# A third turn buffer and three reorderings in an adaLN attention and FFN block

## The chip, the cores and the metric

The kernel runs on one core of a Trainium2 chip. Time is the device time of one execution in microseconds (us), lower is better. All arithmetic is float32.

## The reference

Eight batches (B = 8) of 1024 rows with 256 columns pass through a modulated attention and a modulated feed-forward network, each added back to the row.

```python
mod = (_silu(L0_c) @ L0_wmod).reshape(L0_c.shape[0], 6, 1, -1)
sa, ca, ga, sb, cb, gb = (mod[:, j] for j in range(6))
ga = (2 * (ga >= 0) - 1) * jnp.maximum(jnp.abs(ga), 0.25)     # gb likewise
h = _layernorm(x, axis=-1) * (1 + ca) + sa
scores = jnp.einsum('nsd,ntd->nst', h * w_lhs, h * w_rhs)
x = x + ga * jnp.einsum('nst,ntd->nsd', softmax(scores, axis=2), h)
h = _layernorm(x, axis=-1) * (1 + cb) + sb
x = x + gb * (relu(h @ W1 + b1) @ W2 + b2)
```

## The kernel before

**Tiles and stages.** A batch has eight row tiles of 128 rows (`NT = 8`). The main loop (line 1140) goes over batches `b` and stages `i` from 0 to 7. Stage `i` finishes the attention of row tile `i` of batch `b`, computes the scores of tile `i + 2` (`ahead`), and runs a quarter of the FFN of the half batch that was finished earlier (`fb`, `fg`). Stages 0, 1, 4 and 5 (`first`) do the first FFN product for two pairs of column blocks each, `c` and `c + 1`. Stages 2, 3, 6 and 7 do the second FFN product (`y_first`, `y_second`) and the attention product of two row tiles together (`pair_begin`, `pair_end`). Products over pairs replace eight block products by seven and some sums. The FFN of the last half batches follows in a closing loop (line 1343).

**What sets the order.** `pin` ties each instruction to the one before it on its engine, so that every engine executes its instructions in the order in which the code names them. Engines wait for each other by semaphores that follow from the data and from the reuse of tiles. A tile with `bufs=n` can be written again when all readers of the tile n allocations earlier are done; transfers that read it count as readers. DMAs are issued by SP (`nc.sync`) in order, some loads by ACT.

**Names around the change.** Engines are PE (matmul), DVE (vector), ACT (scalar), POOL (GpSimd) and SP.

- Scores: `direct` (psc, L410) computes one half of the symmetric part; `mirror` (L433) turns it by blocks of 32 on DVE into a tile T (named Tm), and `move` writes T to DRAM (D_m, L304) and reads it back turned (L307).
- T is one tag for four users: the mirrored scores (Tm), the turned norms for attention (T_a) and FFN (T_f, both L320), and the FFN result (T_y, L853). It has two buffers, the number of the pool `two`.
- Softmax: `row_max` (m, L460, DVE), `max_turn` (pm, L465, a PE transpose of the maximum), `subtract` (pT, L472, DVE), `exponent` (pT, L481, ACT), then `product` (po, L493) or the pair products (pp, L544; pq, pr, L584).
- Sides: `prepare_turn_apart` (rT and lT, L340, ACT) makes the next batch's two score operands from X_a, the turned T_a.
- First FFN product: `pair_products` makes pa, pb and pc (L718) and keeps a copy of pa in SBUF (`kept`, L737, ACT, three buffers); `between`, called after pb, is where `max_turn` is put. `pair_sums` (L752 to L761) and `pair_last` add them on DVE (L769) and POOL (L770); `pair_last` first writes one more product over the left half of pa. `pair_relu` (L779, L780) and `pair_turn` (L789 to L792) follow.
- Statistics: `pair_stats` takes mean and variance of two row tiles on DVE (L239, L240), `ffn_rstd` the reciprocal deviation on ACT (rb, L245, L246).

In a stage of the first kind, the order in the code is: `direct(ahead)`, `pair_products(c)` with `max_turn(late)` in it, `pair_sums(c)`, `mirror(ahead)`, `pair_last(c)`, in stage 4 the turn T_a of the next batch, `subtract(late)`, `pair_products(c + 1)`, in stage 5 the next sides, the ReLUs, `exponent(late)`, `pair_sums(c + 1)`, `pair_last(c + 1)`, `row_max(ahead)`. `late` is the tile whose scores were completed in the stage before; in stage 5 it is tile 6.

Of the kernel before, what the change touches and what calls it, by code (L numbers as in the profile page):

```python
# [11 lines left out]
F32 = mybir.dt.float32  # L12
# [5 lines left out]
P = 128  # L18
# [6 lines left out]
def adaln_block_kernel(  # L25
# [14 lines left out]
    B, S, D = x.shape  # L40
    INTER = W1.shape[1]
    NT = S // P
    ND = D // P
    NI = INTER // P
    HALF = 512
    TH = HALF // P
    H2 = HALF // 2
    NH = NI // 2
    V = 32
    NV = P // V  # L50
# [3 lines left out]
    two = ctx.enter_context(tc.tile_pool(name="two", bufs=2))  # L54
    work = ctx.enter_context(tc.tile_pool(name="work", bufs=3))
# [67 lines left out]
    w1 = const.tile([P, ND, INTER], F32, name="w1")  # L123
# [14 lines left out]
    def warm(n):  # L138
# [9 lines left out]
            name=nc.get_next_instruction_name(),  # L148
# [88 lines left out]
    def stats(mv, t, src, name):  # L237
        st = work.tile([P, nc.vector.BN_STATS_DIM], F32, tag="st", name=f"st_{name}")
        nc.vector.bn_stats(st, src)  # L239
        nc.vector.bn_aggr(mv[:, t, :], st)  # L240

    def rstd_of(mv, tag, name):

        r = work.tile([P, TH], F32, tag=tag, name=name)
        nc.scalar.activation(r, mv[:, :, 1], AF.Ln, bias=eps)  # L245
        nc.scalar.activation(r, r, AF.Exp, scale=-0.5)  # L246
        return r
# [50 lines left out]
    def move(out, blocks, m, name, hurry=True):  # L298


        D_ = dram.tile([NV, V, NV, NT * V], F32, tag="D", name=f"D_{name}", bufs=3)
        D_ = D_[:, :, :, 0:m]
        for a in range(NV):
            nc.sync.dma_start(  # L304
                out=D_[:, :, a, :].rearrange("b u m -> u b m"), in_=blocks[ts(a, V)]
            )
        read = lambda: nc.sync.dma_start(out=out, in_=D_.rearrange("b u a m -> (b u) a m"))  # L307
        if hurry:
            read()
            read_back()  # L310
        else:
            reads.append(read)

    def turn_blocks(src, name, X=None):

        T = two.tile([P, NV, NT * V], F32, tag="T", name=f"T_{name}")
        for k in range(ND):
            nc.vector.transpose(  # L320
                T.rearrange("p b (k t v) -> p k b t v", k=ND, v=V)[:, k],
                src(k).rearrange("p t (b v) -> p b t v", v=V),
            )
        if X is None:
            X = two.tile([P, NV, NT * V], F32, tag="X", name=f"X_{name}", bufs=1)
        move(X, T, NT * V, name)
        return X.rearrange("p a (k t v) -> p k t a v", k=ND, v=V)
# [6 lines left out]
    def prepare_turn_apart(b, g, side):  # L334

        tag = "lr"[side] + "T"
        T = two.tile([P, ND, HALF], F32, tag=tag, name=f"{tag}_{b}_{g}", bufs=2)
        (lT_t, rT_t)[side][b, g] = T
        for k in range(ND):
            nc.scalar.activation(  # L340
                T[:, k, :].rearrange("p (t a v) -> p t a v", a=NV, v=V),
                pre[b, g][:, k], AF.Identity,
                scale=side_col(side, 0, k, b), bias=side_col(side, 1, k, b),
            )
# [77 lines left out]
    def mirror(b, i):  # L422
        if i == NT - 1:
            return
        n = NT - 1 - i
        if b == 0:
            mirror_first(i)
            return
        T = two.tile([P, NV, NT * V], F32, tag="T", name=f"Tm_{b}_{i}")
        T = T.rearrange("p b m -> p (b m)")[:, : NV * n * V].rearrange(  # L430
            "p (b m) -> p b m", b=NV
        )
        nc.vector.transpose(  # L433
            T.rearrange("p b (j v) -> p b j v", v=V),
            sc_t[b][:, i + 1 :, :, i, :].rearrange("p j b v -> p b j v"),
        )
        move(
            sc_t[b][:, i, :, i + 1 :, :].rearrange("p a j v -> p a (j v)"), T, n * V,
            f"m{b}_{i}",
        )  # L440
# [39 lines left out]
    def exponent(b, i):  # L480
        nc.scalar.activation(pT_t[b, i], pT_t[b, i], AF.Exp)  # L481
# [134 lines left out]
    def pair_stats(b, i):  # L616
        two_t.pop((b, i))
        g, j = divmod(i, TH)
        for q in range(2):
            stats(mvb_t[b, g], j + q, x_tile(b, i + q), f"b{b}_{i + q}")  # L620
# [15 lines left out]
    def ffn_rstd(b, g):  # L636
        mv = mvb_t.pop((b, g))
        ffn["r", g] = mv, rstd_of(mv, "rb", f"rb_{b}_{g}")
# [75 lines left out]
    lo, hi = slice(0, H2), slice(H2, HALF)  # L714
    pairs = {}

    def mm(out, lhsT, rhs):
        nc.tensor.matmul(out, lhsT=lhsT, rhs=rhs, start=True, stop=True)  # L718

    def pair_products(b, g, c, between=None):  # L720

        if c == 0:
            ffn["f"] = two.tile([P, NI, HALF], F32, tag="f", name=f"f_{b}_{g}", bufs=1)
            if b < B - 1:
                ffn["ft"] = two.tile([P, 3, NH, H2], F32, tag="ft", name=f"ft_{b}_{g}", bufs=1)
        hT, hs = ffn["hT", g]
        n = ts(c, P)
        s1, a22 = (w1[:, k, ds((c + NH) * P, P)] for k in range(2))

        pool, tag = (ps_s, "s") if b == B - 1 else (ps_a, "a")  # L730
        pa = ps_a.tile([P, HALF], F32, tag="a", name=f"pa_{b}_{g}_{c}")
        pb = pool.tile([P, HALF], F32, tag=tag, name=f"pb_{b}_{g}_{c}")
        pc = ps_a.tile([P, HALF], F32, tag="a", name=f"pc_{b}_{g}_{c}")
        mm(pa[:, lo], w1[:, 0, n], hT[:, 0, lo])
        mm(pa[:, hi], s1, hs[:, 0])
        kept = work.tile([P, HALF], F32, tag="kept", name=f"kept_{b}_{g}_{c}", bufs=3)
        nc.scalar.copy(kept, pa)  # L737
        mm(pb[:, lo], w1s[:, 0, n], hs[:, 1])
        mm(pb[:, hi], w1s[:, 1, n], hs[:, 2])
        if between:  # L740
            between()
        mm(pc[:, lo], w1[:, 1, n], hT[:, 1, lo])
        mm(pc[:, hi], a22, hT[:, 0, hi])
        pairs[c] = pa, pb, pc, kept

    def pair_sums(b, g, c):
# [16 lines left out]
    def pair_last(b, g, c):  # L763


        pa, kept, u = pairs.pop(c)
        f = ffn["f"]
        mm(pa[:, lo], w1s[:, 2, ts(c, P)], ffn["hT", g][0][:, 1, hi])
        nc.vector.tensor_tensor(f[:, c, hi], pa[:, lo], u, ALU.add)  # L769
        nc.gpsimd.tensor_tensor(  # L770
            f[:, c::NH, hi],
            f[:, c::NH, hi],
            kept[:, None, hi].to_broadcast([P, 2, H2]),
            ALU.add,
        )
# [72 lines left out]
    def y_turn(b, g, hurry=False):  # L848

        Y = ffn["Y"]  # L850
        T = two.tile([P, NV, NT * V], F32, tag="T", name=f"T_y{b}_{g}")
        for h in range(2):
            nc.vector.transpose(  # L853
                T.rearrange("p a (t h u) -> p a t h u", h=2, u=V)[:, :, :, h, :],
                Y[:, h].rearrange("p (t a v) -> p a t v", a=NV, v=V),
            )
        Y = Y.rearrange("p h r -> p (h r)").rearrange("p (b m) -> p b m", b=NV)
        move(Y, T, NT * V, f"y{b}_{g}", hurry)
        ffn["rows", b, g] = Y.rearrange("p b (t h u) -> p t h b u", h=2, u=V)
# [279 lines left out]
    late = None  # L1139
    for b in range(B):  # L1140
        for i in range(NT):
# [6 lines left out]
            c = i % TH * 2  # L1148

            if (b, i) == (0, NT - 2):  # L1150
# [11 lines left out]
                late, last_exponent = ahead, None  # L1162
# [38 lines left out]
            if first:  # L1201
# [3 lines left out]
                pair_products(fb, fg, c, turn_max)  # L1205
                if i == 0:
                    ffn_rstd(b - 1, 1)
                elif (b, i) == (B - 1, TH):
                    ffn_rstd(b, 0)
                if (b, i) == (1, 0):  # L1210
                    weights(*late)
                    late = None
# [3 lines left out]
                if ahead:  # L1216
                    mirror(*ahead)
                pair_last(fb, fg, c)
                if i == 0 and back:
                    for q in range(2):  # L1220
                        y_add(ub, ug, q)
# [5 lines left out]
                if late:  # L1227
                    subtract(*late)
                pair_products(fb, fg, c + 1, (lambda: max_turn(*extra)) if extra else None)
                if i == 5 and b + 1 < B:  # L1230
                    prepare_turn_apart(b + 1, 1, 1)
                    prepare_turn_apart(b + 1, 1, 0)
                pair_relu(c)
                sides_too = i == 4 and b + 1 < B
                if sides_too:
                    prepare_turn_apart(b + 1, 0, 1)
                if late:
                    exponent(*late)
                if sides_too:
                    prepare_turn_apart(b + 1, 0, 0)  # L1240
# [80 lines left out]
            if first:  # L1321
                product(b, i)
                product_out(b, i)
            elif half and ahead:
                pair_end(b, i - 1)
                pair_out(b, i - 1)
                if i < NT - 1:
                    y_turn(fb, fg)
                if i == NT - 1:
                    assert not queue  # L1330
                    right_sums(b + 1, range(3))
                if i == NT - 1 or b == B - 1:
                    pair_stats(b, i - 1)
            late = ahead if ahead != extra else None
            if first and back:
# [6 lines left out]
    b = B - 1  # L1342
# [75 lines left out]
```

## Time and profile before

| what | value |
|---|---|
| median of 3 runs | 772.51 us (772.37 to 774.09) |
| profiled execution | 774.46 us, its span 772.7 us |
| granted TensorE clock | 1.0 of full speed throughout |
| PE busy | 759.6 us in 3708 matmuls |
| DVE busy | 565.1 us |
| POOL busy | 538.2 us |
| ACT busy | 375.4 us |
| DMA | 95.18 MB, 123 GB/s on the mean |

The profile is of one execution, recorded by the hardware. A line of the timeline gives the start and the duration of a group of equal instructions, the engine, the line of the kernel, the operation, what it writes and reads, the shape, and in brackets how long the engine had been idle before and whose end released it. Ends of matmuls are modelled; their starts are recorded. The second number of a waits row is how often, the third how long the longest was.

### The profile page before, as it was taken

To read this page: it belongs to the slowest core of one execution; us is meant where nothing else is said; L and a number is where in the kernel's file an instruction comes from. 1 tells how busy PE (TensorE), PEld (TensorE's weight loads), DVE (VectorE), ACT (ScalarE), POOL (GpSimd) and SP (SyncE) were. 2 spreads that over 40 slices of the span, in tenths; PEclk is the share of its full clock that TensorE was granted. 3 is DMA by queue.
4 is the path that set the end of the run, shared out by engine and by line. 5 is a ranking of instruction groups with operands and counts; after the bars stand their busy time and mean duration, and the time that the engine had idled before them with its cause. 6 is when DMAs were issued, how large, how long until landed. Compare 5 with 4: busy or idle time off the path is not lost.

```text
span 772.7 us, 11479 instructions
## 1 busy us (share of the span) xinstructions
PE 759.6 (98%) x3708; PEld 621.8 (80%) x3708; DVE 565.1 (73%) x1222; ACT 375.4 (49%) x681; POOL 538.2 (70%) x632
## 2 busy tenths in 40 slices
PE   8999999999999999999999999999999999999998
PEld 3576788788887888778887888878888788889886
DVE  6697878768785887758787687876878677595632
ACT  3464546635456355645546444563546535251511
POOL 4543974978849686596867787497884969559641
PEclk9999999999999999999999999999999999999999
DMA  5314335356443554434543554436534254142220
GB/s 193 123 50 145 106 103 133 101 176 170 123 122 101 171 143 113 140 95 151 156 126 118 150 150 130 117 101 192 167 93 130 87 167 142 35 115 98 81 83 27
DMA packets 106211, 95.18 MB, mean 123 GB/s; under 512 B 29700, under 2 KB 98848, under 8 KB 106152
## 3 DMA queue, kind: packets, MB, share of 16 engines
q1 hardware_dynamic: 98408, 85.81, 38.0%
q10 hardware_dynamic: 7744, 8.65, 3.7%
q8 instruction: 29, 0.48, 0.3%
q14 instruction: 30, 0.25, 0.1%
HBM read 50.62 MB, written 43.81 MB: 122 GB/s over the span
## 4 chain that ended last, share of the span: by engine, by line
PE 78%; DVE 10%; POOL 4%; DMA 3%; issue 2%; SPq 1%; ACT 1%; DVEq 0%; POOLq 0%
PE psc L410 14%; PE po L493 12%; PE pa L718 7%; PE yc L796 6%; PE ya L796 6%; PE yb L796 6%; PE pc L718 5%; PE pr L584 5%; PE pb L718 4%; PE pq L584 3%; PE py L901 3%; PE yd L796 3%; PE pp L544 3%; DMA D_y<-T_y 2%; DVE pT L472 1%
## 5 line engine op out<-in xcount | busy, mean ns | idle before, releaser
L770 POOL TENSOR_TENSOR f<-f,kept 128x512 f32<-128x512 f32 x64 | 81.5, 1273 | 116.7 <-DVE f L769 84.6
L410 PE MATMUL psc<-rT,lT 128*128 128x512 f32 (+3 forms) x384 | 134.6, 487 | 0.0
L493 PE MATMUL po<-xg,pT 128*128 128x257 f32 x576 | 131.6, 380 | 0.0
L493 PEld LDWEIGHTS po<-xg,pT 128*128 128x128 f32 x576 | 108.9, 190 | 15.9 <-issue 1.0
L472 DVE TENSOR_TENSOR pT<-sc,pm 128x1024 f32<-128x1024 f32 x64 | 77.1, 1205 | 30.7 <-PE pm L465 24.8
L410 PEld LDWEIGHTS psc<-rT,lT 128*128 128x128 f32 x384 | 67.7, 191 | 37.9 <-issue 26.3
L417 ACT COPY sc<-psc 128x512 f32<-128x512 f32 (+3 forms) x96 | 44.9, 475 | 104.0 <-PE psc L410 94.5
L481 ACT ACTIVATE pT<-pT 128x1024 f32<-128x1024 f32 x64 | 67.3, 1052 | 33.8 <-DVE pT L472 33.8
L460 DVE TENSOR_REDUCE m<-sc 128x1 f32<-128x1024 f32 x64 | 77.3, 1207 | 0.0
L737 ACT COPY kept<-pa 128x512 f32<-128x512 f32 x64 | 37.4, 584 | 78.2 <-PE pa L718 78.2
L779 ACT ACTIVATE f<-f 128x512 f32<-128x512 f32 x64 | 40.1, 627 | 62.4 <-POOL f L770 62.4
L718 PE MATMUL pb<-hs,w1s 128*128 128x256 f32 x256 | 66.0, 380 | 0.9 <-DVE f L755 0.8
L718 PE MATMUL pc<-hT,w 128*128 128x256 f32 x256 | 65.8, 380 | 0.0
L634 POOL TENSOR_TENSOR x<-x,rows 128x256 f32<-128x256 f32 x64 | 45.3, 739 | 22.3 <-DVE x L509 11.8
L718 PEld LDWEIGHTS pb<-hs,w1s 128*128 128x128 f32 x256 | 47.8, 190 | 9.1 <-DVE f L755 2.0
L718 PEld LDWEIGHTS pc<-hT,w 128*128 128x128 f32 x256 | 46.7, 192 | 6.9
L796 PE MATMUL yc<-f,w2s 128*128 128x256 f32 x224 | 52.1, 379 | 0.0
L796 PEld LDWEIGHTS yc<-f,w2s 128*128 128x128 f32 x224 | 41.5, 190 | 10.1 <-issue 2.9
L433 DVE STREAM_TRANSPOSE Tm<-sc 128x896 f32<-128x896 f32 (+6 forms) x49 | 34.6, 707 | 13.3 <-ACT sc L417 12.4
L790 POOL TENSOR_TENSOR ft<-ft,f 128x256 f32<-128x256 f32 x56 | 40.8, 728 | 4.4
L791 POOL TENSOR_TENSOR ft<-ft,f 128x256 f32<-128x256 f32 x56 | 40.8, 728 | 4.4
L789 POOL TENSOR_TENSOR ft<-f 128x256 f32<-128x256 f32 x56 | 40.9, 731 | 0.0
(165 smaller groups left out, 1672.7 us busy)
## 6 DMA issues: line engine op xcount, KB each, us to landing
D_f<-T_f SPq DMA_DIRECT2D x60, 128.0 KB, 2.7
X_f<-D_f SPq DMA_DIRECT2D x15, 512.0 KB, 3.7
D_a<-T_a SPq DMA_DIRECT2D x56, 128.0 KB, 3.2
D_y<-T_y SPq DMA_DIRECT2D x56, 128.0 KB, 2.6
Y<-D_y SPq DMA_DIRECT2D x14, 512.0 KB, 3.5
out_dram<-x SPq DMA_DIRECT2D x14, 512.0 KB, 3.0
X_a<-D_a SPq DMA_DIRECT2D x13, 512.0 KB, 3.4
x<-in_L_attn_x_dram ACTq DMA_DIRECT2D x12, 512.0 KB, 4.6
```

The source lines that it names most:

```text
L410: nc.tensor.matmul(psc[:, : hi - lo], lhsT=lT_t[b, i // TH][:, k, ts(i % TH, P)], rhs=rT_t[b, n][:, k, lo - n * HALF : HALF], start=(k == ...
L417: nc.scalar.copy(score_row(b, i)[:, lo // V : hi // V, :], psc[:, : hi - lo].rearrange("p (n v) -> p n v", v=V),)
L460: nc.vector.tensor_reduce(m, score_row(b, i), AX.XY, ALU.max)
L472: nc.vector.tensor_tensor(pT.rearrange("p j (a v) -> p j a v", v=V), score_columns(b, i), pm[:, :P].rearrange("p (j a v) -> p j a v", j=1, ...
L481: nc.scalar.activation(pT_t[b, i], pT_t[b, i], AF.Exp)
L493: nc.tensor.matmul(po[:, : D + 1], lhsT=pT[:, t, :], rhs=xg_t[b][:, t, 0 : D + 1], start=(t == 0), stop=(t == NT - 1),)
L584: nc.tensor.matmul(out, lhsT=lhs[:, t, :], rhs=rhs[:, t, :], start=(t == 0), stop=(t == TH - 1),)
L634: queue.append(lambda: nc.gpsimd.tensor_tensor(out, in0, row, op))
L718: nc.tensor.matmul(out, lhsT=lhsT, rhs=rhs, start=True, stop=True)
L770: nc.gpsimd.tensor_tensor(f[:, c::NH, hi], f[:, c::NH, hi], kept[:, None, hi].to_broadcast([P, 2, H2]), ALU.add,)
L789: add(ft[:, 0, c], f[:, c + NH, hi], f[:, c, hi], ALU.subtract)
L796: nc.tensor.matmul(out, lhsT=lhs(c), rhs=rhs(c), start=(c == 0), stop=(c == NH - 1))
```

## The change

Five edits. The tag T gets three buffers in all of its uses. In `pair_products`, `between` is called after both pc products and not ahead of them. In stage 5, `exponent(late)` stands ahead of the next batch's sides. In the last batch, the statistics of tiles 2 and 3 and the reciprocal deviation of the first half stand in stage 4 behind the first pair's sums; before, the statistics stood at the end of stage 3, and the deviation ahead of the sums. To make room, `kept` has two buffers for three, and in the last batch's own FFN (the closing loop) the third pair of each four (c = 2) uses the tile `s1`.

```diff
 # turn_blocks, mirror, y_turn
-        T = two.tile([P, NV, NT * V], F32, tag="T", name=...)
+        T = two.tile([P, NV, NT * V], F32, tag="T", name=..., bufs=3)
 # pair_products
-        kept = work.tile([P, HALF], F32, tag="kept", name=f"kept_{b}_{g}_{c}", bufs=3)
+        tag, bufs = ("s1", 1) if b == B - 1 and c % 3 == 2 else ("kept", 2)
+        kept = work.tile([P, HALF], F32, tag=tag, name=f"kept_{b}_{g}_{c}", bufs=bufs)
         nc.scalar.copy(kept, pa)
         mm(pb[:, lo], w1s[:, 0, n], hs[:, 1])
         mm(pb[:, hi], w1s[:, 1, n], hs[:, 2])
+        mm(pc[:, lo], w1[:, 1, n], hT[:, 1, lo])
+        mm(pc[:, hi], a22, hT[:, 0, hi])
         if between:
             between()
-        mm(pc[:, lo], w1[:, 1, n], hT[:, 1, lo])
-        mm(pc[:, hi], a22, hT[:, 0, hi])
 # main loop, stages 0, 1, 4, 5
                 if i == 0:
                     ffn_rstd(b - 1, 1)
-                elif (b, i) == (B - 1, TH):
-                    ffn_rstd(b, 0)
...
                 pair_last(fb, fg, c)
+                if (b, i) == (B - 1, TH):
+                    pair_stats(b, 2)
+                    ffn_rstd(b, 0)
...
-                if i == 5 and b + 1 < B:
-                    prepare_turn_apart(b + 1, 1, 1)
-                    prepare_turn_apart(b + 1, 1, 0)
+                if i == 5:
+                    exponent(*late)
+                    if b + 1 < B:
+                        prepare_turn_apart(b + 1, 1, 1)
+                        prepare_turn_apart(b + 1, 1, 0)
                 pair_relu(c)
...
-                if late:
+                if late and i != 5:
                     exponent(*late)
 # main loop, stages 3 and 7
-                if i == NT - 1 or b == B - 1:
+                if i == NT - 1:
                     pair_stats(b, i - 1)
```

More of the change, by code (lines that the diff above doesn't have):

```diff
@@ L314, in turn_blocks @@
     def turn_blocks(src, name, X=None):
-        T = two.tile([P, NV, NT * V], F32, tag="T", name=f"T_{name}")
+        T = two.tile([P, NV, NT * V], F32, tag="T", name=f"T_{name}", bufs=3)
         for k in range(ND):
@@ L428, in mirror @@
             return
-        T = two.tile([P, NV, NT * V], F32, tag="T", name=f"Tm_{b}_{i}")
+        T = two.tile([P, NV, NT * V], F32, tag="T", name=f"Tm_{b}_{i}", bufs=3)
         T = T.rearrange("p b m -> p (b m)")[:, : NV * n * V].rearrange(
@@ L850, in y_turn @@
         Y = ffn["Y"]
-        T = two.tile([P, NV, NT * V], F32, tag="T", name=f"T_y{b}_{g}")
+        T = two.tile([P, NV, NT * V], F32, tag="T", name=f"T_y{b}_{g}", bufs=3)
         for h in range(2):
```

## The prediction

> **What bounds the kernel.** I read the engine table first, then the chain of waits, then the timelines around each place the diff touches.
>
> ```profile
> PE 759.6 (98%) x3708; PEld 621.8 (80%) x3708; DVE 565.1 (73%) x1222; ACT 375.4 (49%) x681; POOL 538.2 (70%) x632
> ...
> PE 78%; DVE 10%; POOL 4%; DMA 3%; issue 2%; SPq 1%; ACT 1%; DVEq 0%; POOLq 0%
> ```
>
> TensorE (PE) is full; time can only come from the moments at which it stands still. After 100 us the timeline has few: only from there does it pay to look. The first kind, in batch 2 (stage 5):
>
> ```profile
> 225.90 1.03 PE L718 MATMUL pb<-hs,w1s 128*128 128x256 f32 x4
> 227.12 0.32 PE L465 MATMUL pm<-ident,m 128*128 128x128 f32 x1 [0.18 <-DVE m L460]
> 227.28 1.03 PE L718 MATMUL pc<-hT,w 128*128 128x256 f32 x4
> ...
> 221.56 1.31 DVE L320 STREAM_TRANSPOSE T_a<-xg 128x512 f32<-128x512 f32 x2 [1.56 <-DMA D_y<-T_y]
> 225.85 1.21 DVE L460 TENSOR_REDUCE m<-sc 128x1 f32<-128x1024 f32 x1
> ```
>
> The maximum's transpose `pm` waits for the row maximum, itself 1.56 us late because T_a waits for a turn buffer. The bracket says 0.18, but printed matmul ends are modelled and overlap the next start, so I count from start to start. Where nothing waits, pb to pm to pc takes 0.86 + 0.11 (same stage, batch 7); here it takes 1.22 + 0.16. The cost is 0.42, not 0.18. Then batch 3, with batch 6 below it:
>
> ```profile
> 314.85 1.31 DVE L320 STREAM_TRANSPOSE T_a<-xg 128x512 f32<-128x512 f32 x2 [3.29 <-DMA D_y<-T_y]
> 316.10 0.61 PE L410 MATMUL psc<-rT,lT 128*128 128x128 f32 x4
> 318.23 0.70 PE L718 MATMUL pa<-hT,w 128*128 128x256 f32 x2 [1.52 <-DVE f L755]
> ...
> 602.70 1.52 ACT L340 ACTIVATE rT<-X_a,sides 128x512 f32<-128x512 f32 x2 [3.89 <-DMA X_a<-D_a]
> 603.60 3.60 PE L410 MATMUL psc<-rT,lT 128*128 128x512 f32 x8
> 606.58 1.04 ACT L481 ACTIVATE pT<-pT 128x1024 f32<-128x1024 f32 x1
> 607.67 1.16 PE L544 MATMUL pp<-xg,pT 128*128 128x129 f32 x8 [0.48 <-ACT pT L481]
> ```
>
> Batch 3: the same buffer wait, 3.29, holds the pair sums on VectorE (DVE), and PE. Batch 6: ScalarE (ACT) waits 3.89 for a transfer with tile 6's exponential queued behind it, and the pair product waits for that. Last, batch 7:
>
> ```profile
> 678.56 0.39 DVE L239 BATCH_NORM_STATS2 st_b<-x 128x6 f32<-128x256 f32 x1
> 680.17 0.48 DVE L755 SCALAR_TENSOR_TENSOR f<-pb,b_step,u 128x256 f32<-128x256 f32 x1
> 680.71 1.13 PE L718 MATMUL pb<-hs,w1s 128*128 128x256 f32 x4 [0.79 <-DVE f L755]
> 682.54 0.59 PE L718 MATMUL pa<-hT,w1s 128*128 128x256 f32 x2
> ...
> 679.72 0.30 ACT L245 ACTIVATE rb<-mvb,eps 128x4 f32<-128x4 f32 x1 [2.31 <-DVE mvb L240]
> 680.16 0.57 ACT L737 COPY kept<-pa 128x512 f32<-128x512 f32 x1
> ```
>
> Four statistics instructions stand ahead of the pair's sums; PE's next `pb` waits for them.
>
> **What the Trainium skill says.** "Perfetto Trace Analysis", Optimization Strategy: a gap that repeats on the engine that should be saturated can mean too little memory for the next tile. The trace agrees: the 0.42 returns in six batches, behind waits of T_a for T_y's writes (11.6 us over 6). "DMA: Bandwidth & Descriptors", Latency and other measured facts: HBM access grows under load. The landing of D_y ranges here from 2.0 to 3.9 us, so I treat the size of buffer waits as varying between executions. "TensorE: Matmul & The Clock Gate", The mechanism: matmuls start and end in program order. Here pc starts 0.16 us after the late pm, and all behind it moves.
>
> **The change, part by part.** The order of instructions on each engine shows what moves: on PE, `pm` behind both `pc` products in stages 0, 1, 4 and 5 of batches 1 to 7; on ACT, seven exponentials; on DVE, four statistics. POOL's and SP's orders stay, so no transfer is issued past another. No work is added.
>
> *Third turn buffer.* T_a then waits for writes issued a stage earlier, long landed. DVE gets 1.56 us earlier in batch 2's stage 4, so the maximum ends near 225.5, before pb's end at 226.8. The sums that held PE in batches 3 and 5 are no longer late: start to start, psc to pa takes 2.13 and 0.99 instead of 0.44, and the next step 0.53 instead of 0.43. This gives 1.79 + 0.65 = 2.44 us. X_a comes no sooner: SP issues D_a behind two read-backs (593.30 and before, D_a at 593.85), after T_a had ended at 591.4.
>
> *Transpose a product later.* Removes the wait of six batches a second time: 0.87 us of pc covers 0.42. With the buffer it is one gain, not two: 0.38 in batch 1, 0.42 to 0.47 in the five others, sum 2.5. Cost: subtract gets pm 0.87 later, nothing, because DVE does the pair's sums and the sum of `pa` first, whose product follows pm on PE. If that cover were gone, it would be 0.87 in each of the 29 places, on DVE.
>
> *Tile 6's exponential ahead of the sides.* Its input ended at 599.9 in batch 6, so it runs in the 3.89 us of waiting. psc to pp took 4.07 against 3.43, and the next step 1.00 against 0.89: gain 0.75, that batch alone. Queued behind it on ACT are rT, lT and the ReLUs. Where the transfer is early, rT starts up to 1.06 later; in batch 6 rT ends at 604.2 and its first reader starts near 605.3, so nothing to at most a few tenths; I take 0.
>
> *Two `kept` buffers for three.* The copy of pair c+2 then waits for POOL's addition of pair c. The least slack I find is 2.34 us (stage 5, second copy); in the closing loops c = 2 uses the s1 tile and keeps the distance at three. 0.
>
> *Last batch's statistics behind the sums.* The sums start 1.05 earlier, L755 ends at 679.6, before pb's turn at 679.76. Gone are 0.95 + 0.11 = 1.06 us. But ACT keeps its order: rb stands ahead of the second `kept`. The statistics now end at 681.92 (0.18 for the last aggregate), rb's two steps take 0.44 to the copy's start, the copy 0.57: it ends at 682.96. The product `pa<-hT,w1s` writes what that copy reads. Its turn is 682.54 - 1.06 = 681.48; it starts at 683.02. A new wait of 1.54, with 0.1 for the restart 1.64. Behind it PE is 0.58 later than before, while X_f on ACT is 0.4 earlier and with it the DVE and POOL work; so PE no longer waits at 690 (0.07 + 0.11) and at 706 for POOL's sums (0.28 + 0.11). Net: -1.06 + 1.64 - 0.18 - 0.39 = 0.0. Bounds of the new wait: 0, if the copy were in time, and 2.0.
>
> *Sum.* 2.44 + 2.5 + 0.75 + 0.0 = 5.7 us. The profiled execution took 774.46 (span 772.7 and 1.76 around it): **768.8**. The median of the three runs is 772.51, 1.95 less. Buffer and exponential waits vary: without those 3.19, an execution of the old kernel would take 771.3. So I think that the median holds about 1.2 of them, and that the new kernel, having none, gains 3.7 against it.
>
> **Rivals.** *A, the median holds none of the varying waits:* then 772.5 - 2.5 = 770.0, and up to 771.4 if the new kernel has others of that kind. For it: three waits in six batches are few. Against it: two runs of 772.4 and one of 774.1 look like more or fewer of such waits.
>
> *B, the copy comes in time:* then 1.64 less, though the POOL wait of 0.39 stays: 767.6. Against it: rb stands ahead of the copy in ACT's order.
>
> *C, the change doesn't do what it says:* the maximum is held by other DVE work, not by T_a, and only the 0.87 of cover helps partly; half of 2.5 and little else: 771.3. Against it: DVE runs from T_a to the maximum without an idle bracket.
>
> *D, slower:* the shorter kept ring. Its place is stage 5, where `kept` of the fourth pair would wait for POOL's addition of the second (ending 227.35 in batch 2, copy at 229.69), and PE behind it (copy ends 230.28, product at 231.16). Slack is 2.34 + 0.88 = 3.2 us. Each us beyond costs 6 (batches 1 to 6): from 4.2 us late the gain is gone and 774.8 is reached, at 4.5 it is 776.6. Against it: that addition waits for DVE, which gets earlier.
>
> **Numbers.** About 0.3%, 2.3 us, is what a measurement can tell from no change: the borders are 770.2 and 774.8. Forecast (768.0 to 769.9): 0.60. A: 0.22, half of it under 770.2. B: 0.08. C: 0.06. D: 0.04. Faster 0.60 + 0.11 + 0.08 = 0.79, same 0.17, slower 0.04. The range 767.5 to 771.4 takes in B's end, all the bounds of the new wait, and most of A.
>
> **What the new profile would show.** No T_a waiting for D_y; no bracket at pm in stage 5; batch to batch (the ya product of stage 2) 91.1 us each, where it was 91.5 to 93.3; exponential directly behind the second `kept`; in batch 7, no wait at pb, and one of about 1.4 us at pa<-hT,w1s for kept. I am wrong if batches still take 91.5, if T_a waits for another transfer, or if the wait in batch 7 is absent.

## The result, and the profile after

The changed kernel takes 769.62 us (median of 6 runs, 769.39 to 770.54); the kernel before 772.44 (6 runs, 771.67 to 774.09). The ratio is 0.9961, 95% interval 0.9948 to 0.9974: faster by 2.8 us at the medians, by 2.0 to 4.0 within the interval. The profiled execution took 769.46, its span 767.7.

The engine table and the chain of waits of the changed kernel:

```profile
PE 756.5 (99%) x3708; PEld 621.7 (81%) x3708; DVE 566.0 (74%) x1222; ACT 375.0 (49%) x681; POOL 538.9 (70%) x632
...
PE 93%; DVE 3%; POOL 1%; issue 1%; ACT 1%; DMA 1%; SPq 0%; DVEq 0%; POOLq 0%
```

The same work is done; the chain now runs along PE for 93% of the span, where it was 78%. The DMA share fell from 3% to 1%. The beginnings of the second FFN product in stage 2 (the chain of waits in order of time: start, duration, what) give the length of a batch. First the kernel before, then the changed one:

```profile
104.79 1.73 PE ya L796 x8
196.27 1.73 PE ya L796 x8
```

```profile
105.42 1.73 PE ya L798 x8
196.53 1.73 PE ya L798 x8
```

The six distances of this kind were 91.5 to 93.3 us before and are 91.11 each now. The first line stood at 104.79 before and stands at 105.42 now: 0.63 us were lost ahead of it. Stage 5 of batch 2, from the timeline:

```profile
224.46 1.21 DVE L460 TENSOR_REDUCE m<-sc 128x1 f32<-128x1024 f32 x1
226.12 1.03 PE L718 MATMUL pb<-hs,w1s 128*128 128x256 f32 x4
226.99 1.03 PE L718 MATMUL pc<-hT,w 128*128 128x256 f32 x4
227.85 0.27 PE L465 MATMUL pm<-ident,m 128*128 128x128 f32 x1
230.51 1.06 ACT L481 ACTIVATE pT<-pT 128x1024 f32<-128x1024 f32 x1 [0.42 <-DVE pT L472]
```

The maximum ends at 225.67, well ahead of pb's end. Tile 6's exponential ends at 231.57, before the next sides begin at 233.08, which still wait 1.51 us for X_a. Batch 7 shows the wait that the change adds, behind rb on ACT:

```profile
675.60 1.03 PE L718 MATMUL pc<-hT,w 128*128 128x256 f32 x4
676.92 0.30 ACT L245 ACTIVATE rb<-mvb,eps 128x4 f32<-128x4 f32 x1 [4.48 <-DVE mvb L240]
677.36 0.57 ACT L739 COPY kept<-pa 128x512 f32<-128x512 f32 x1
677.98 0.70 PE L718 MATMUL pa<-hT,w1s 128*128 128x256 f32 x2 [1.36 <-ACT kept L739]
```

And the first stage of batch 1 shows one that the prediction did not have. First the kernel before, then the changed one:

```profile
80.82 0.27 PE L465 MATMUL pm<-ident,m 128*128 128x128 f32 x1
81.13 1.22 DVE L472 TENSOR_TENSOR pT<-sc,pm 128x1024 f32<-128x1024 f32 x1 [1.88 <-PE pm L465]
82.27 0.48 DVE L752 SCALAR_TENSOR_TENSOR u<-pb,cols,kept 128x256 f32<-128x256 f32 x1
83.39 1.13 PE L718 MATMUL pb<-hs,w1s 128*128 128x256 f32 x4
```

```profile
81.45 0.27 PE L465 MATMUL pm<-ident,m 128*128 128x128 f32 x1
81.76 1.22 DVE L472 TENSOR_TENSOR pT<-sc,pm 128x1024 f32<-128x1024 f32 x1 [2.74 <-PE pm L465]
82.90 0.48 DVE L754 SCALAR_TENSOR_TENSOR u<-pb,cols,kept 128x256 f32<-128x256 f32 x1
84.02 1.13 PE L718 MATMUL pb<-hs,w1s 128*128 128x256 f32 x4 [1.00 <-DVE f L757]
```

Here, and at no other of the 29 places, the subtraction stands ahead of the pair's sums on DVE (`weights(*late)` directly behind the pair's products). pm comes later, so do the subtraction and the sums, and the second pair's pb waits. PE was 0.24 us earlier than in the profile before when it came to this stage (nearly all of it since 11 us, ahead of everything that the change touches) and is 0.63 later behind it: 0.87 us, the length of the two pc products.

### The profile page after: what moved, and what is told of

It is laid out like the page before. It is cut to its first block, busy times and chain, and to the rows that moved or that the text cites. A ratio compares the mean times of both kernels' runs of the same rounds, so it can differ in the third digit from the quotient of the medians.

```text
span 767.7 us, 11489 instructions
## 1 busy us (share of the span) xinstructions
PE 756.5 (99%) x3708; PEld 621.7 (81%) x3708; DVE 566.0 (74%) x1222; ACT 375.0 (49%) x681; POOL 538.9 (70%) x632
## 4 chain that ended last, share of the span: by engine, by line
PE 93%; DVE 3%; POOL 1%; issue 1%; ACT 1%; DMA 1%; SPq 0%; DVEq 0%; POOLq 0%
PE po L493 16%; PE psc L410 15%; PE pa L718 10%; PE pb L718 7%; PE pc L718 7%; PE yc L798 6%; PE ya L798 6%; PE yb L798 6%; PE pr L584 5%; PE pq L584 3%; PE pp L544 3%; PE py L903 3%; PE yd L798 3%; PE pm L465 1%; POOL xg L285 1%
## 5 line engine op out<-in xcount | busy, mean ns | idle before, releaser
L718 PEld LDWEIGHTS pc<-hT,w 128*128 128x128 f32 x256 | 48.6, 190 | 6.6
```

## The experiments

Times are medians; ratios are against the kernel before on the same chip, with their 95% intervals. The kernel before had medians of 773.93, 773.37 and 772.90 in the three groups (37, 27 and 10 runs), so the kernels of one group are best compared with each other. "Extra" below is the time between two starts on PE, less the least time that the same two steps take elsewhere in the trace. Where two numbers are added, the second is the step behind the wait, which is 0.10 to 0.11 longer in these traces.

### Group 1: each edit by itself

**Statistics back.** The changed kernel with the edit to the last batch's statistics undone.

```diff
+                elif (b, i) == (B - 1, TH):
+                    ffn_rstd(b, 0)
...
-                if (b, i) == (B - 1, TH):
-                    pair_stats(b, 2)
-                    ffn_rstd(b, 0)
...
-                if i == NT - 1:
+                if i == NT - 1 or b == B - 1:
                     pair_stats(b, i - 1)
```

> The changed kernel with the last batch's statistics and deviation where they were before. Theory: the new wait for kept in batch 7 (1.52 + 0.11) goes and the old waits at pb (1.06), at 690 (0.18) and 706 (0.39) return, so the edit is worth nothing: 769.5, within 0.3 of the changed kernel's 769.6. Rival: the waits at 690 and 706 had other causes and stay away, then 769.1; or the edit was a gain of 1 us, then 770.6.

Measured: 769.57 (0.9951, 0.9939 to 0.9963). The extras are 1.06 at pb in batch 7, 0.19 at the next stage's pb and 0.41 at the pair product: 1.66 together, against 1.63 at pa<-hT,w1s in the changed kernel. The edit exchanges waits, as forecast.

**Deviation later.** The changed kernel, with `ffn_rstd` of batch 7 behind the second pair's copy.

```diff
-                    ffn_rstd(b, 0)
...
                 pair_products(fb, fg, c + 1, (lambda: max_turn(*extra)) if extra else None)
+                if (b, i) == (B - 1, TH):
+                    ffn_rstd(b, 0)
```

> The changed kernel with only the deviation rb of batch 7 moved behind the second pair's copy on ACT; the statistics stay behind the sums. Theory: the wait of pa<-hT,w1s for kept (1.63) is ACT's order, not DVE's lateness; it goes, and at most 0.39 comes back at the pair product that waits for POOL: 768.0 to 768.4. Rival: the copy is late for another reason, or rb, now later, holds X_f and the next transfers: 769.6 or more.

Measured: 769.44 (0.9950, 0.9938 to 0.9962), no better. The wait for kept is gone, so ACT's order was its cause. But PE now comes to the pair products of stage 6 too early; the timeline of this kernel:

```profile
698.35 1.27 POOL L564 TENSOR_TENSOR s<-pT 128x512 f32<-128x512 f32 x1
699.67 1.16 PE L584 MATMUL pr<-tsum,s 128*128 128x128 f32 x8
699.69 1.27 POOL L565 TENSOR_TENSOR pT<-pT,pT 128x512 f32<-128x512 f32 x1
701.02 1.16 PE L584 MATMUL pr<-tsum,pT 128*128 128x128 f32 x8 [0.19 <-POOL pT L565]
701.04 1.33 POOL L566 TENSOR_TENSOR pT<-s,pT 128x512 f32<-128x512 f32 x1
702.42 1.83 PE L584 MATMUL pq<-tsum,pT 128*128 128x129 f32 x14 [0.25 <-POOL pT L566]
```

Each product waits for one of POOL's sums, which begin at 698.35 here and at 698.29 in the changed kernel: they did not get earlier. POOL's timeline shows no idle time from 680.2 up to them in either kernel. Extras: 0.46 + 0.51 + 0.11 here and 0.26 at the pb before. Of 1.63 taken away, 1.34 came back. My limit of 0.39 took the old size of this wait for its greatest.

**Later transpose alone.** The kernel before with only `between` behind the pc products.

```diff
+        mm(pc[:, lo], w1[:, 1, n], hT[:, 1, lo])
+        mm(pc[:, hi], a22, hT[:, 0, hi])
         if between:
             between()
-        mm(pc[:, lo], w1[:, 1, n], hT[:, 1, lo])
-        mm(pc[:, hi], a22, hT[:, 0, hi])
```

> The kernel before with pm behind both pc products, nothing else. Theory: the six waits at pm in stage 5 (2.5 together) go without the third buffer, since 0.87 us of pc covers 0.42; the first stage of batch 1 gets worse by 0.87, because there the subtraction stands ahead of the pair's sums; T_a still waits for T_y's writes. 772.4 - 2.5 + 0.9 = 770.8, batches at 91.1 where T_a's wait is short. Rival: pm only passes the wait on to what comes behind it, and the kernel stays at 772.4 or rises to 773.3.

Measured: 773.25 (1.0000, 0.9993 to 1.0008; the means of all runs, 773.66 and 773.73, are closer than the medians): no gain, the rival's outcome. The wait at pm is gone, and an extra of 0.31 to 0.37 stands in each of the six batches at the pb of the next pair instead (see the two-buffer run below). The first stage of batch 1 got worse, as forecast: its second pb has an extra of 1.16 + 0.11, where the kernel before has 0.30 + 0.11. Only the place of the transpose differs.

**Third buffer alone.** The kernel before with the third turn buffer and the shorter kept ring.

```diff
-        T = two.tile([P, NV, NT * V], F32, tag="T", name=...)
+        T = two.tile([P, NV, NT * V], F32, tag="T", name=..., bufs=3)
...
-        kept = work.tile([P, HALF], F32, tag="kept", name=..., bufs=3)
+        tag, bufs = ("s1", 1) if b == B - 1 and c % 3 == 2 else ("kept", 2)
+        kept = work.tile([P, HALF], F32, tag=tag, name=..., bufs=bufs)
```

> The kernel before with three turn buffers and the shorter kept ring with s1, nothing else. Theory: the six waits at pm go as well (2.5), because the maximum comes 1.5 us earlier, and so do the varying waits for D_y; batch 1's first stage stays good; batch 7's 1.06 stays. 772.4 - 2.5 - 0.6 (varying) = 769.3, between 769.0 and 769.9. Rival: the maximum is held by other DVE work, and only the varying part goes: 771.8.

Measured: 771.45 (0.9976, 0.9967 to 0.9985), single runs from 770.16 to 773.88. All six waits at pm are gone, and T_a's as well. The time is above my window because of the exponential: in the profiled execution, three of six batches wait for it, 2.9 us together. Batch 3 of this kernel:

```profile
324.44 1.52 ACT L340 ACTIVATE rT<-X_a,sides 128x512 f32<-128x512 f32 x2 [4.21 <-DMA X_a<-D_a]
328.32 1.04 ACT L481 ACTIVATE pT<-pT 128x1024 f32<-128x1024 f32 x1
329.41 0.82 PE L544 MATMUL pp<-xg,pT 128*128 128x129 f32 x5 [0.80 <-ACT pT L481]
```

### Group 2: the pairs of edits, and the ring

**Exponential alone.** The kernel before with tile 6's exponential ahead of the sides.

```diff
+                if i == 5:
+                    exponent(*late)
...
-                if late:
+                if late and i != 5:
                     exponent(*late)
```

> The kernel before with tile 6's exponential ahead of the next sides, nothing else. Theory: it takes away only a wait that some executions have (0.75 in one batch of the profiled one): 772.4 - (0 to 0.8) = 772.0, pm waits of 0.42 in six batches stay and batches stay at 91.5 or more. Rival: it pushes the sides back and the scores wait: 772.6 to 773.5.

Measured: 772.00 (0.9985, 0.9975 to 0.9995), faster by 1.4 at the medians (0.4 to 1.9 by the interval of the ratio), where 0 to 0.8 was expected. Its 13 runs lie between 771.5 and 773.0; the 27 of the kernel before, in the same group, between 771.8 and 775.6. No wait for the exponential is in its trace; the pm waits are there.

**Two turn buffers.** The changed kernel without the third buffer.

```diff
-        T = two.tile([P, NV, NT * V], F32, tag="T", name=..., bufs=3)
+        T = two.tile([P, NV, NT * V], F32, tag="T", name=...)
```

> The changed kernel with two turn buffers again (kept ring as changed). Theory: pm behind pc covers the regular wait, so batches are at 91.1 except where D_y's writes land late; the cost is only the varying part, 0 to 1.2 us on the mean: 770.0, with a wider spread between executions than the changed kernel's. Rival: the buffer carries the whole 2.5 and the pm move nothing: 772.1.

Measured: 772.88 (0.9994, 0.9986 to 1.0002). The theory was wrong: the buffer is worth 3.3 us (against 769.62 and 769.52 for the changed kernel in other groups), though pm's place covers the wait at pm. The wider spread that I expected is not there either: the 13 runs lie within 0.8 us. Stage 5 of batch 2 of this kernel shows where the wait went:

```profile
226.72 1.21 DVE L460 TENSOR_REDUCE m<-sc 128x1 f32<-128x1024 f32 x1
228.50 0.27 PE L465 MATMUL pm<-ident,m 128*128 128x128 f32 x1
229.62 0.48 DVE L757 SCALAR_TENSOR_TENSOR f<-pb,b_step,u 128x256 f32<-128x256 f32 x1
230.16 1.13 PE L718 MATMUL pb<-hs,w1s 128*128 128x256 f32 x4
```

pm has no wait. But DVE as a whole is late by the time T_a lost, so the sums behind the maximum are late too: L757 ends at 230.10, and pb, whose turn was 229.90, starts at 230.16. No bracket is printed, since the modelled end of the product before (230.06) lies only 0.10 ahead of this start; the extra is 0.26 + 0.10. Such extras add up to 2.1 us in the six batches. A further 1.0 is lost in batch 5, where T_a waits 2.50 for D_y and PE waits for the sums behind it.

**The kept ring without s1.** The changed kernel with two `kept` buffers in the closing loop too.

```diff
-        tag, bufs = ("s1", 1) if b == B - 1 and c % 3 == 2 else ("kept", 2)
+        tag, bufs = "kept", 2
```

> The changed kernel with two kept buffers everywhere, without the s1 tile in the closing loop. In the trace of before, four copies there start 0.9 to 1.1 us ahead of the end of POOL's addition two pairs earlier. Theory: those copies wait about 1 us each, but the product that needs the copy is a whole pair later on PE, so 0 to 1 us comes through: 769.6 to 770.6. Rival: the waits add up on PE, 4 x 1 us: 773.

Measured: 769.63 (0.9954, 0.9942 to 0.9966), the changed kernel's time. Four copies in the closing loop wait for POOL's additions, as expected, but no product on PE waits for them. In the changed kernel itself none of the 64 copies waits for POOL. The shorter ring costs nothing, with or without s1.

**Both mended.** The changed kernel with the deviation later (as above) and, in the first stage of batch 1, both maxima's pm ahead of pc.

```diff
-    def pair_products(b, g, c, between=None):
+    def pair_products(b, g, c, between=None, early=False):
...
+        if between and early:
+            between()
         mm(pc[:, lo], w1[:, 1, n], hT[:, 1, lo])
         mm(pc[:, hi], a22, hT[:, 0, hi])
-        if between:
+        if between and not early:
             between()
...
-                pair_products(fb, fg, c, turn_max)
+                pair_products(fb, fg, c, turn_max, (b, i) == (1, 0))
...
-                pair_products(fb, fg, c + 1, (lambda: max_turn(*extra)) if extra else None)
+                pair_products(fb, fg, c + 1, (lambda: max_turn(*extra)) if extra else None, bool(extra))
```

> The changed kernel with two things mended: in batch 7 the deviation rb behind the second copy (as in the run that moves it alone), and in the first stage of batch 1 the maxima turned ahead of pc as before. Theory: -1.63 + up to 0.39 and -0.87 of PE waits: 767.1 to 767.5, faster than both kernels. Rival: batch 1's wait is not from the later transpose, then about 768.2.

Measured: 768.50 (0.9941, 0.9929 to 0.9953), above the forecast by the same 1 us of POOL waits, and faster than both kernels.

### Group 3: what carries the gain

**Third buffer and exponential.** The kernel before with these two edits (diffs above).

> The kernel before with two of the edits: the third turn buffer (with the shorter kept ring and s1) and tile 6's exponential ahead of the sides. Theory: these two carry the whole gain; the later transpose costs 0.87 in the first stage of batch 1 and brings nothing once the buffer is there, and the statistics edit is worth 0. So 769.6 - 0.9 = 768.7, and little spread. Rival: the later transpose is needed beside the buffer, then waits at pm are back and the time is 770 or more.

Measured: 768.72 (0.9944, 0.9932 to 0.9956), runs from 768.2 to 769.3. With the buffer there and pm in its old place, the timeline of batch 2 has no wait at pm:

```profile
223.24 1.21 DVE L460 TENSOR_REDUCE m<-sc 128x1 f32<-128x1024 f32 x1
224.91 1.03 PE L718 MATMUL pb<-hs,w1s 128*128 128x256 f32 x4
225.77 0.27 PE L465 MATMUL pm<-ident,m 128*128 128x128 f32 x1
225.88 1.03 PE L718 MATMUL pc<-hT,w 128*128 128x256 f32 x4
```

From start to start, pb to pm takes 0.86 and pm to pc 0.11, the undisturbed distances.

**Mended, transpose early everywhere.** The run "deviation later" with pm ahead of pc in all stages, as in the kernel before.

```diff
+        if between:
+            between()
         mm(pc[:, lo], w1[:, 1, n], hT[:, 1, lo])
         mm(pc[:, hi], a22, hT[:, 0, hi])
-        if between:
-            between()
```

> The changed kernel with the deviation rb behind the second copy, and pm ahead of pc in all stages, as before. Theory: the same as the kernel that keeps the old place in the first stage of batch 1 alone, 768.5 within 0.2, since no other stage profits from the later place. Rival: stage 5 profits by 0.42 in six batches, then 771.

Measured: 768.56 (0.9939, 0.9927 to 0.9951). The two yardsticks of this group, without a new edit:

> The changed kernel itself, on the same chip as the other three, as their yardstick: 769.6.

> The kernel with both mended, again, on the same chip: 768.5, 1.1 under the changed kernel and 0.3 under the one with buffer and exponential alone.

Measured: 769.52 (0.9953, 0.9941 to 0.9965) for the changed kernel, 768.50 (0.9938, 0.9924 to 0.9951) for the one with both mended. So three kernels with pm early in batch 1's first stage lie at 768.5 to 768.7, and the changed kernel 0.8 to 1.0 above them. The buffer and the exponential carry the whole gain; the later transpose adds nothing to them and costs what batch 1 loses.

## Why the prediction was right, and where it was not

The prediction was 768.8, the measurement 769.62, the gain 2.8 instead of 3.7 us. The gain is the weaker of the two readings: it hangs on which executions of the kernel before were drawn, and in group 3 the same two kernels lie 3.4 apart at the medians. The sum was made for the profiled execution, and there the gain was 5.00 (774.46 to 769.46) instead of 5.7: 0.87 was lost in batch 1, and 0.24 won at the start, which is luck: the scores that begin at 76.52 in the kernel before begin at 76.28 in the changed kernel, and between 75.94 and 76.76 in all the traces. By the steps:

- **Counting from start to start: right.** The brackets alone gave 0.18 for a wait at pm; the batches got shorter by 0.4 where nothing else had been wrong (91.48 and 91.55 to 91.11), as the starts said.
- **Third buffer: right in kind, and worth more than its share.** I gave it 2.44 us of varying waits and let it divide 2.5 with the transpose. The two-buffer run and the transpose alone show that the 2.5 is nearly all the buffer's.
- **The transpose "removes the wait of six batches a second time": wrong.** It covers pm, but what waits for DVE behind it is the next pair's pb, 0.31 to 0.37 per batch where pm's wait was about 0.42. In the changed kernel this error does no harm, because the buffer is there; but beside the buffer the edit brings nothing at all.
- **The transpose's cost, "nothing, because DVE does the pair's sums and the sum of `pa` first": the step that failed.** It holds in 28 of the 29 places. In the first stage of batch 1 the subtraction stands ahead of the sums, and the cost is 0.87, the value that I named for lost cover. It explains the difference between 768.8 and 769.6. The prediction had set aside the timeline ahead of 100 us, and this stage lies at 79 to 85. The run with both mended and the later-deviation run differ only by the place of the two maxima's transposes in that stage, and by 0.94 us at the medians (two groups); the extra at the second pb there is 1.16 + 0.11 in the one and 0.30 + 0.10 in the other. In group 3, pm early everywhere gives the same 768.56.
- **Exponential: right in kind, too small.** 0.75 in one execution; alone it gains 1.4 at the medians of 13 and 27 runs, and with the buffer 2.7 (771.45 to 768.72, in two groups). My reading that the median holds 1.2 us of varying waits came from three values, and the size of these waits differs from run to run. Why the edit is worth more beside the buffer was not tested.
- **Last batch: right to 0.01.** The new wait was put at 1.64 and is 1.52 + 0.11; the waits at 690 and 706 went; the net is 0.0, and undoing the edit gives 769.57 against 769.62.
- **Rivals.** The time lies in the forecast's range (768.0 to 769.9). A's 770.0 is nearer than 768.8, but not for its reason: the executions of the kernel before do hold varying waits, as the gain of the exponential alone shows. B's copy in time was made by moving rb, and its 0.39 of POOL was 1.08. C is refuted by the third buffer alone, where pm waits for nothing. D: even without s1 the ring costs nothing.

Left open: why the waits for X_a and D_y vary from one execution to the next. The traces show where X_a's lateness enters. In stage 5 of the kernel before, X_a takes 3.15 to 3.30 us from issue to landing in all six batches; in batch 6, the one that loses time, it is issued late, at 599.42, because D_a stands on SP behind the read-back of the scores. That read-back comes 4.36 us after the first write of D_m there, and 3.03 in batch 2. In the run with the third buffer alone, X_a itself takes 3.9 and 4.8 us in two of the three batches that wait.

## What to carry to other kernels

On an engine that is full, measure each wait by the distance between starts, then ask which engine is late as a whole: shifting the one instruction that shows the wait hands the wait to the next one, and only removing the cause (here a buffer) moves the time. Check an argument of the form "something else comes first" at every place where the helper is called, the special first iteration above all. When a wait is taken away, ask what the bound engine meets next: here 1.34 of 1.63 us came back, 1.08 of it as waits for POOL's sums.

## What the runs showed of the hardware that I had not expected

The spread of a kernel's time is itself a reading. The kernels with tile 6's exponential behind the sides spread widely: the kernel before over 3.7 us in 37 runs (771.9 to 775.6), the later transpose alone over 3.5 in 22, the third buffer alone over 3.7 in 15. The kernels with it ahead of the sides do not: the exponential alone spreads over 1.5 us in 13 runs, the two-buffer kernel over 0.8 in 13, the changed kernel over 1.2 in 11 (769.4 to 770.5). So most of the spread came from one ACT instruction per batch that was queued behind a transfer landing at varying times.
